# Keys and values of an attention kernel computed with features on partitions, values matmuls unjoined

## The chip, the cores and the metric

The kernel runs on one core of one Trainium2 chip. Its time is the device time of one execution in microseconds (us); the time of a kernel is the median of several executions. Beside it stands one execution recorded by the hardware profiler, whose span is counted from the first to the last instruction.

## The reference

Attention with 16 query heads and one shared head for keys and values, 64 batches of 128 tokens, width 512, head size 64, all in fp32. A null key and a null value stand ahead of each batch's own.

```python
xn = layernorm(x, g_in)
q = (xn @ Wq).reshape(b, n, H, DH).transpose(0, 2, 1, 3) * scale
kv = xn @ Wkv
k, v = (kv[..., :DH], kv[..., DH:])          # one head for all queries
k = jnp.concatenate([nk, k], axis=1)         # null key and null value first
v = jnp.concatenate([nv, v], axis=1)
sim = jnp.einsum('bhid,bjd->bhij', q, k) + bias
# causal mask, then the mask of valid tokens
attn = jax.nn.softmax(sim, axis=-1)
out = jnp.einsum('bhij,bjd->bhid', attn, v)
out = out.transpose(0, 2, 1, 3).reshape(b, n, INNER) @ Wo
return x + layernorm(out, g_out)
```

The kernel subtracts the null key from every key and the null value from every value (so the null score is zero and the null value is added back once at the end). That subtraction is the only arithmetic between the keys' and values' matmuls and their use.

## The kernel before

**Stages.** 64 batches are worked in 16 groups of four and in 32 pairs. A *turn* d handles the pair of batches 2d and 2d+1: `turn(d)` makes their scores on PE (`scores`, L661), adds bias and mask on DVE (`scores_add`), and runs the values matmuls (`values`, L785) of the pair before. Then `body(d)` fills PE with everything else: keys and values for one pair of the next group (`kv_pair`), seven block products that give the next group's queries (`product`, `inner_product`), and seven block products of the output projection for the pair before (`out_product`). Turns 1 to 29 run so; `body_first` is turn 0's, and the last turns have code of their own (`turn_end`, `body_end`, `body_last`). Ahead of turn 0 stands a prologue that computes group 0 (its queries in chunks, `q_half` and `q_batches`), written out step by step at the end of the kernel.

**What sets the order.** The order is written by hand: each engine executes its own instructions in the order in which the program issues them, and the framework adds semaphore waits where two instructions touch the same buffer. Nearly all DMAs are issued on SP's queue, in program order as well. PSUM is handed out by tags with few buffers: `ps_s` "s" (one), `ps_q` "a" and "c", `ps_y` "X" and "Y" (one each) and `ps_w` "w" (two). A product that continues in a room (`start=False`) must wait until the copy of what stands there is done: product 6 on "a" is copied by ACT (`keep`, L551, the tile ku), then product 7 adds into the same "a".

**Keys and values.** For each batch, `kv_mm` (L348) holds the tokens (xT, 128 x 128) as weights and moves the 128 columns of Wkv, four chunks of the contraction. The result has tokens on partitions and 128 features (64 of keys, 64 of values) in the free dimension. `kv_pair` does two batches into two halves of one "s" room; `kv_pair_out` (L395) subtracts the null vectors (broadcast over all partitions, `nkv`) in one DVE operation into `kvt`. In the second pair of each group, that is in odd turns, follow

- `values_to_memory` and `values_spread`: values go to DRAM by three DMAs and come back by four, which put each 32-token block's values on all four quadrants of partitions (`vr`);
- `keys_T`: a DVE transpose of 32 x 32 blocks (L424, `kb`), three DMAs to DRAM and four back into `kT`, with features on partitions, twice (rows 0 to 63 and 64 to 127).

In fp32 each matmul of the program shows as two records in the profile, so a pair's 8 matmuls are 16 records.

**Around the pair in `body`.** On DVE the pair's output comes after the maxima and statistics of other batches and before `pair_nmr` (L943), `norm_stats`, `scores_max`, `inner_out` (L621), and the output of the query products (`q_out`, L560). On ACT, `values_out` (L824) comes before it, then `keep` of product 1 (L551, kp), `pair_norm` (L950, which needs `pair_nmr`'s result), exponentials (L707), `out_keep` (L906), and `keep` of product 6 (L551, ku).

**Values.** `values` works on 32-row quadrants of the array. For each quadrant s there are four positions in `turns`, each with a block of keys j, a target `to` and a count n of blocks. A quadrant named in `wide` joins two matmuls of j = 1 (128 columns each) into one of 256 columns. In turns 2 to 29, quadrant 3 is joined; in turn 1 and in the last turns nothing is.

`PLACE = 0, 1, 3, 2` is the order in which the four 32-token blocks of a batch lie in xT.

Of the kernel before, what the change touches and what calls it, by code (L numbers as in the profile page):

```python
# [8 lines left out]
FP = mybir.dt.float32  # L9
U8 = mybir.dt.uint8  # L10
AF = mybir.ActivationFunctionType
# [6 lines left out]
def kernel(  # L18
# [127 lines left out]
    nkv = const.tile([P, KVN], FP, name="nkv")  # L146
# [115 lines left out]
    xT, qT, kT, vr = {}, {}, {}, {}  # L262
# [85 lines left out]
    def kv_mm(m, pkv=None):  # L348
        g, t = divmod(m, GB)
        if pkv is None:  # L350
            pkv = ps_w.tile([P, KVN], FP, tag="w", name=f"pkv_{m}")
        for kc in range(KC):
            nc.tensor.matmul(  # L353
                pkv,
                xT[g][:, t, kc, :],
                wkv[:, kc, :],
                start=(kc == 0),
                stop=(kc == KC - 1),
            )
        return pkv  # L360

    def kv_pair(m):

        pkv = ps_s.tile([P, 2, DIM], FP, tag="s", name=f"pkv_{m}")
        for i in range(2):
            kv_mm(m + i, pkv[:, i, 0:KVN])
        return pkv

    def to_tokens(out, places):
        for at, to, n in ((0, 0, 2), (2, 3, 1), (3, 2, 1)):  # L370
            nc.sync.dma_start(
                out=out[to * Q : (to + n) * Q], in_=places[at * Q : (at + n) * Q]
            )

    kvts, vds = {}, {}

    def kv_tile(g):
        kvts[g] = hp.tile([P, 2, GB, DH], FP, tag="kv", name=f"kvt_{g}", bufs=1)

    def values_to_memory(g):  # L380
        vds[g] = dp.tile([P, GB * DH], FP, tag="vd", name=f"vd_{g}")
        to_tokens(vds[g], kvts[g][:, 1].rearrange("p t d -> p (t d)"))

    def kv_out(m, pkv):
        g, t = divmod(m, GB)
        if t == 0:
            kv_tile(g)
        nc.vector.tensor_tensor(
            kvts[g][:, :, t, :],
            pkv.rearrange("p (r d) -> p r d", r=2),  # L390
            nkv.rearrange("p (r d) -> p r d", r=2),
            ALU.subtract,
        )

    def kv_pair_out(m, pkv):  # L395
        g, t = divmod(m, GB)
        if t == 0:
            kv_tile(g)
        nc.vector.tensor_tensor(
            kvts[g][:, :, t : t + 2, :],  # L400
            pkv[:, :, 0:KVN].rearrange("p i (r d) -> p r i d", r=2),
            nkv.rearrange("p (r d) -> p r d", r=2)
            .unsqueeze(2)
            .broadcast_to([P, 2, 2, DH]),
            ALU.subtract,
        )
        if t == GB - 2:
            values_to_memory(g)

    def values_spread(g):  # L410

        vd = vds.pop(g)
        vr[g] = hp.tile([P, NQ, GB, DH], FP, tag="vr", name=f"vr_{g}")
        src = vd.rearrange("(j p) e -> p j e", p=Q)
        for s in range(NQ):
            nc.sync.dma_start(
                out=vr[g][s * Q : (s + 1) * Q].rearrange("p j t d -> p j (t d)"),
                in_=src,
            )

    def keys_T(g):

        kb = hp.tile([P, 2, GB, Q], FP, tag="kb", name=f"kb_{g}", bufs=1)
        nc.vector.transpose(  # L424
            kb,
            kvts[g][:, 0].rearrange("p t (c k) -> p c t k", k=Q),
        )
        kd = dp.tile([P, 2, GB * Q], FP, tag="kd", name=f"kd_{g}")
        to_tokens(kd.rearrange("p c e -> p (c e)"), kb.rearrange("p c t q -> p (c t q)"))
        if g == 0:  # L430
            load_mask(0)
        kT[g] = hp.tile([P, NQ, GB, Q], FP, tag="kT", name=f"kT_{g}", bufs=1)
        src = kd.rearrange("(i p) c e -> c p i e", p=Q)
        for s in range(NQ):
            nc.sync.dma_start(
                out=kT[g][s * Q : (s + 1) * Q].rearrange("p i t q -> p i (t q)"),
                in_=src[s % 2],
            )
# [222 lines left out]
    def scores(b, hf, tiles=None):  # L661
# [10 lines left out]
        for f in range(NF):  # L672
            for r in range(2):
                rows = slice(r * DH, (r + 1) * DH)
                for u in range(2):
# [3 lines left out]
                        kT[g][rows, 0 : nk // Q, t, :],  # L679
# [105 lines left out]
    def values(b, wide=()):  # L785
# [8 lines left out]
        for turn in range(len(turns[0])):  # L794
            for s in range(NQ):
# [7 lines left out]
                for r in range(2):  # L803
# [3 lines left out]
                        vr[g][quad, j, t, :],  # L807
# [172 lines left out]
    def turn(d):  # L980
# [16 lines left out]
        values(p, () if d == 1 else (3,))  # L997
        values(p + 1, () if d == 1 else (3,))
# [270 lines left out]
    def body(d):  # L1269
# [258 lines left out]
    q_half(4, 0)  # L1528
# [4 lines left out]
    q_half(5, 0)  # L1533
# [3 lines left out]
    q_half(6, 0)  # L1537
# [3 lines left out]
    q_half(7, 0)  # L1541
# [105 lines left out]
```

## Time and profile before

| | before |
|---|---|
| median of 3 runs | 1028.9 us (1028.81 to 1029.09) |
| profiled execution | 1028.83 us |
| its span | 1027.1 us |
| granted TensorE clock | 1.000 |
| instructions | 31399 |

How to read it. Engines are PE (matmul), PEld (load of weights, which overlaps PE), DVE (VectorE), ACT (ScalarE), POOL (GpSimd) and SP (which issues DMAs; SPq is its queue). L805 is line 805 of the kernel. A row of the timeline has the start, the duration from the first start to the last end of merged instructions, engine, line, operation, tiles written and read, their shapes, the count, and in brackets the idle time of the engine ahead of it and what ended it. Durations of neighbours overlap, since an instruction starts before the one before it has drained; so costs are taken from start to start. A row of groups has count, busy time and mean duration, then idle time and its releaser. A row of one tile has minimum, median and maximum duration. A row of waits has who waited for whom, the total in us, the number of times and the longest. A row of stretches has its length, then PE, PEld, DVE, ACT and POOL busy time with counts, the granted clock, and DMA. A row of DMA issues ends in the median us from issue to landing.

### The profile page before, as it was taken

The numbers are of one execution on the slowest core, as the hardware profiler recorded it, in microseconds if no ns is written. First come the engines' busy times: TensorE is split into PE (matmuls) and PEld (weight loads), VectorE is DVE, ScalarE is ACT, GpSimd is POOL, SyncE is SP. The second block draws the span as 40 slices with busy tenths as digits, with TensorE's granted clock in tenths as the row PEclk, the third lists the DMA queues.
The fourth block names the chain that finished last, engine by engine and source line by source line (L and its number), as shares of the span: only waits on it lengthen the run. The fifth ranks groups of instructions, "written<-read, shape, count | busy, mean of one in ns | idle before, by whom it ended". The sixth has DMA issues, their size and how long they took to land.

```text
span 1027.1 us, 31399 instructions
## 1 busy us (share of the span) xinstructions
PE 1017.6 (99%) x12337; PEld 904.7 (88%) x12337; DVE 787.5 (77%) x1774; ACT 677.5 (66%) x2709; POOL 745.4 (73%) x579
## 2 busy tenths in 40 slices
PE   9999999999999999999999999999999999999997
PEld 8888888888888888898888888888888888888886
DVE  6867777877778877788777778777788777877697
ACT  4756667666677666686656776666776667856582
POOL 4997768686685867758677686766868678586676
PEclk9999999999999999999999999999999999999999
DMA  7514152241613315133151521415223161330211
GB/s 221 167 33 141 63 171 80 71 120 64 181 69 104 97 63 178 63 120 113 40 170 63 160 85 47 150 63 176 75 94 106 58 184 62 109 88 24 94 64 63
DMA packets 69228, 105.14 MB, mean 102 GB/s; under 512 B 9044, under 2 KB 33496, under 8 KB 67288
## 3 DMA queue, kind: packets, MB, share of 16 engines
q1 hardware_dynamic: 68784, 102.73, 31.9%
q8 instruction: 97, 1.59, 0.6%
q14 instruction: 51, 0.42, 0.1%
q10 hardware_dynamic: 296, 0.40, 0.1%
HBM read 67.45 MB, written 35.65 MB: 100 GB/s over the span
## 4 chain that ended last, share of the span: by engine, by line
PE 97%; DVE 1%; POOL 1%; issue 0%; DMA 0%; POOLq 0%; DVEq 0%
PE pa L539 20%; PE pyX L892 20%; PE pyY L892 10%; PE pc L539 10%; PE po L805 7%; PE pkv L353 6%; PE pyw L892 5%; PE pl L605 4%; PE pq L474 3%; PE ps L676 3%; PE sc_X L676 2%; PE sc_Y L676 2%; PE py_s L892 1%; PE sc_a L676 1%; PE sc_w L676 1%
## 5 line engine op out<-in xcount | busy, mean ns | idle before, releaser
L707 ACT ACTIVATE s<-s,nmax 128x65 f32<-128x65 f32 (+1 forms) x1024 | 371.8, 367 | 62.0 <-DVE nmax L698 62.0
L729 POOL TENSOR_TENSOR s<-s,rinv 128x512 f32<-128x512 f32 (+1 forms) x132 | 190.8, 1447 | 156.3 <-DVE rinv L725 156.3
L641 POOL TENSOR_TENSOR s<-biasp,mneg 128x1552 f32<-128x1552 f32 (+1 forms) x65 | 205.8, 3169 | 51.2 <-DVE s L691 38.2
L707 ACT ACTIVATION_READ_ACCUMULATOR s<-s,nmax 128x1 f32 x1024 | 194.2, 190 | 0.0
L557 ACT COPY qT<-pa 128x256 f32<-128x256 f32 x59 | 22.0, 373 | 155.1 <-PE pa L539 155.1
L698 DVE TENSOR_REDUCE nmax<-s 128x8 f32<-128x1032 f32 (+1 forms) x128 | 121.6, 951 | 0.1
L539 PE MATMUL pa<-xS,wq 128*128 128x256 f32 x472 | 121.2, 379 | 0.0
L745 DVE STREAM_TRANSPOSE sb<-s 128x1536 f32<-128x1536 f32 (+1 forms) x68 | 113.6, 1673 | 2.0 <-POOL s L729 2.0
L892 PE MATMUL pyX<-wo,oT 128*128 128x256 f32 x464 | 109.7, 379 | 0.0
L892 PE MATMUL pyX<-wT,oT 128*128 128x256 f32 x464 | 109.7, 379 | 0.0
L539 PEld LDWEIGHTS pa<-xS,wq 128*128 128x128 f32 x472 | 86.4, 190 | 11.9 <-issue 0.2
L892 PEld LDWEIGHTS pyX<-wo,oT 128*128 128x128 f32 x464 | 86.0, 190 | 10.5
L892 PEld LDWEIGHTS pyX<-wT,oT 128*128 128x128 f32 x464 | 85.9, 190 | 10.6
L872 POOL TENSOR_TENSOR oT<-oT 128x512 f32<-128x512 f32 x64 | 80.6, 1279 | 3.9 <-PE pyw L892 1.6
L805 PE MATMUL po<-sb,vr 32*64 32x128 f32 (+1 forms) x3840 | 81.5, 310 | 0.0
L560 DVE TENSOR_TENSOR qT<-pc,ku 128x256 f32<-128x256 f32 x118 | 48.7, 413 | 39.0 <-PE pc L539 22.5
L805 PEld LDWEIGHTS po<-sb,vr 32*64 32x64 f32 x3840 | 71.3, 131 | 8.1 <-issue 5.7
L824 ACT ACTIVATE oT<-po,nv 128x512 f32<-128x512 f32 (+1 forms) x127 | 73.7, 653 | 0.1
L621 DVE TENSOR_TENSOR qT<-pl,kp 128x128 f32<-128x128 f32 x112 | 31.0, 277 | 55.6 <-PE pl L605 53.8
L280 POOL TENSOR_TENSOR rstd<-rstd,nhalf 128x1 f32<-128x1 f32 x64 | 35.4, 560 | 45.9 <-DVE rstd L279 43.7
L353 PE MATMUL pkv<-wkv,xT 128*128 128x128 f32 x512 | 65.2, 281 | 0.0
L551 ACT COPY ku<-pa 128x256 f32<-128x256 f32 x118 | 43.4, 368 | 32.7 <-PE pa L539 24.4
(185 smaller groups left out, 2395.1 us busy)
## 6 DMA issues: line engine op xcount, KB each, us to landing
res<-in_x_dram SPq DMA_DIRECT2D x64, 256.0 KB, 2.9
x<-in_x_dram SPq DMA_DIRECT2D x63, 256.0 KB, 4.5
out_dram<-y SPq DMA_DIRECT2D x63, 256.0 KB, 2.0
xd<-xb SPq DMA_DIRECT2D x14, 1024.0 KB
xT<-xd SPq DMA_DIRECT2D x56, 256.0 KB, 5.9
vr<-vd SPq DMA_DIRECT2D x64, 128.0 KB, 2.7
kT<-kd SPq DMA_DIRECT2D x64, 64.0 KB, 2.2
wo<-in_L_cond_Wo_dram SPq DMA_DIRECT2D x1, 2048.0 KB, 13.5
```

Of the source, the lines that this page charges most:

```text
L353: nc.tensor.matmul(pkv, xT[g][:, t, kc, :], wkv[:, kc, :], start=(kc == 0), stop=(kc == KC - 1),)
L539: nc.tensor.matmul(prod[tag], w[:, kc, f * P : (f + 1) * P], t[:, :, kc, :], start=(start and kc == 0), stop=(kc == HK - 1), skip_group_ch ...
L641: nc.gpsimd.tensor_tensor(S[b][:, :, keys], biasp[:, :, keys], mneg[:, t, keys] .unsqueeze(1) .broadcast_to([P, R8, keys.stop - keys.start ...
L676: nc.tensor.matmul(home[r][u * DH : (u + 1) * DH, f, :], qT[g, f, t // 2][rows, t % 2, hf, u], kT[g][rows, 0 : nk // Q, t, :], start=True, ...
L698: nc.vector.tensor_reduce(nmax[b][:, hf], S[b][:, :, WITH_NULL[hf]], AX.X, ALU.max, negate=True)
L707: nc.scalar.activation(row, row, AF.Exp, bias=nmax[b][:, hf, k : k + 1], accum_out=rsum[b][:, hf, k : k + 1],)
L729: nc.gpsimd.tensor_tensor(sv, sv, rinvs[b, hf][:, lo:hi].unsqueeze(2).broadcast_to([P, hi - lo, sv.shape[2]]), ALU.mult,)
L745: nc.vector.transpose(sbs[b][:, :, lo:hi].rearrange("p j e q -> p e j q"), S[b][:, lo:hi, 1 : ROW - 1].rearrange("p e (j k) -> p e j k", k=Q),
L805: nc.tensor.matmul(po[s][rows, to : to + n], vr[g][quad, j, t, :], sb[quad, slots, r * NF : (r + 1) * NF, :], start=(turn == 0), stop=True ...
L824: nc.scalar.activation(to, src, AF.Identity, bias=nv2)
L872: eng.tensor_tensor(o, a, b, op)
L892: nc.tensor.matmul(prod[key], h[:, c, :], w[:, c, :], start=(start and c == 0), stop=(c == HC - 1), skip_group_check=not start,)
```

## The change

1. **Matmuls of keys and values.** `kv_pair` now holds Wkv's chunk (128 x 128) as weights and moves the tokens of two batches, 256 columns. The result has the 128 features on partitions (keys on rows 0 to 63, values on rows 64 to 127) and the two batches' tokens in the free dimension, in one half of the "s" room. `kv_mm`, `kv_out`, `to_tokens`, `keys_T` and the rest of the old path are gone.
2. **Keys.** They come out as the scores need them. DVE subtracts the null key for token blocks 0 and 1, ACT (two activations with a bias of minus the null key) for blocks 2 and 3, which change places; one DMA copies rows 0 to 63 to rows 64 to 127. `kT` is one tile for all groups.
3. **Values.** DVE subtracts the null value on rows 64 to 127 into `vTs`; once a group DVE transposes 32 x 32 blocks of these 64 rows x 512 columns (`values_T`), two DMAs write them to DRAM in pieces of 32 features, four bring them back into `vr`.
4. The null vectors are loaded as one value per partition instead of a broadcast row, and `null_negative` computes the negative once.
5. **Values matmuls**: quadrant 3 is no longer joined.
6. **Prologue**: the second pair of group 0 is done as a pair, in a `ps_w` room; query chunks 3 to 7 of the first half use `q_batches` (per batch, 128 columns) instead of `q_half` (256 columns); `load_mask(0)` is issued ahead of `values_T(0)`.

```diff
-    nkv = const.tile([P, KVN], FP, name="nkv")
+    nkv = const.tile([P, 1], FP, name="nkv")
+    nkv_neg = const.tile([P, 1], FP, name="nkv_neg")
...
-            out=nkv, in_=cond[0:2].rearrange("r d -> (r d)").partition_broadcast(P)
+            out=nkv, in_=cond[0:2].rearrange("r d -> (r d)").unsqueeze(1)
...
+    K_ROWS, V_ROWS = slice(0, DH), slice(DH, P)
+    kT = hp.tile([P, NQ, GB, Q], FP, tag="kT", name="kT", bufs=1)
+    vTs = {}
+
+    def kv_pair(m, room=None):
...
+        if room is None:
+            two = ps_s.tile([P, 2, DIM], FP, tag="s", name=f"pkv_{m}")
+            pkv = two[:, 0, 0 : 2 * N]
+        else:
+            pool, tag = room
+            pkv = pool.tile([P, 2 * N], FP, tag=tag, name=f"pkv_{m}")
         for kc in range(KC):
             nc.tensor.matmul(
                 pkv,
-                xT[g][:, t, kc, :],
                 wkv[:, kc, :],
+                xT[g][:, t : t + 2, kc, :],
...
     def kv_pair_out(m, pkv):
         g, t = divmod(m, GB)
         if t == 0:
-            kv_tile(g)
-        nc.vector.tensor_tensor(
-            kvts[g][:, :, t : t + 2, :],
...
+            vTs[g] = hp.tile([P, GB, N], FP, tag="kv", name=f"vT_{g}", bufs=1)
+        two = slice(t, t + 2)
+        nc.vector.tensor_scalar(
+            vTs[g][V_ROWS, two],
+            pkv[V_ROWS].rearrange("p (t n) -> p t n", t=2),
+            nkv[V_ROWS],
+            None,
             ALU.subtract,
         )
...
+        src = pkv[K_ROWS].rearrange("p (t i q) -> p t i q", t=2, i=NQ)
+        out = kT[K_ROWS, :, two].rearrange("p i t q -> p t i q")
+        nc.vector.tensor_scalar(
+            out[:, :, 0:2], src[:, :, 0:2], nkv[K_ROWS], None, ALU.subtract
+        )
+        for i in (2, 3):
+            nc.scalar.activation(
+                out[:, :, i], src[:, :, PLACE[i]], AF.Identity, bias=nkv_neg[K_ROWS]
+            )
+        nc.sync.dma_start(out=kT[V_ROWS, :, two], in_=kT[K_ROWS, :, two])
+
+    def values_T(g):
+
+        vb = hp.tile([P, GB * NQ, Q], FP, tag="vb", name=f"vb_{g}", bufs=1)
+        nc.vector.transpose(
+            vb[V_ROWS], vTs[g][V_ROWS].rearrange("p t (j q) -> p (t j) q", q=Q)
+        )
+        vd = dp.tile([Q, GB * NQ, DH], FP, tag="vd", name=f"vd_{g}")
+        for at in range(0, DH, Q):
+            nc.sync.dma_start(
+                out=vd[:, :, at : at + Q], in_=vb[DH + at : DH + at + Q]
+            )
+        vr[g] = hp.tile([P, GB, NQ, DH], FP, tag="vr", name=f"vr_{g}")
         for s in range(NQ):
             nc.sync.dma_start(
...
+                out=vr[g][s * Q : (s + 1) * Q].rearrange("p t j d -> p (t j) d"),
+                in_=vd,
             )
...
-        values(p, () if d == 1 else (3,))
-        values(p + 1, () if d == 1 else (3,))
+        values(p)
+        values(p + 1)
...
             if h == 1:
-                keys_T(g)
-                values_spread(g)
+                values_T(g)
...
-    pkvs = [kv_mm(m) for m in (2, 3)]
+    pkv2 = kv_pair(2, (ps_w, "w"))
     norm_stats(5)
     norm_stats(6)
+    null_negative()
     kv_pair_out(0, pkv)
     norm_stats(7)
     causal(1)
-    q_half(3, 0)
-    for m in (2, 3):
-        kv_out(m, pkvs[m - 2])
-    keys_T(0)
-    values_to_memory(0)
-    values_spread(0)
+    q_batches((3,))
+    kv_pair_out(2, pkv2)
+    load_mask(0)
+    values_T(0)
...
-    q_half(4, 0)
+    q_batches((4,))
...
-    q_half(5, 0)
+    q_batches((5,))
...
-    q_half(6, 0)
+    q_batches((6,))
...
-    q_half(7, 0)
+    q_batches((7,))
```

The scores read `kT` without the group's index, and `values` reads `vr[g][quad, t, PLACE[j], :]` instead of `vr[g][quad, j, t, :]`.

More of the change, by code (lines that the diff above doesn't have):

```diff
@@ L260 @@
     dp = ctx.enter_context(tc.tile_pool(name="dp", bufs=2, space=bass.MemoryType.DRAM))
-    xT, qT, kT, vr = {}, {}, {}, {}
+    xT, qT, vr = {}, {}, {}
     stats = {}
@@ L360, in kv_mm, with null_negative @@
         return pkv
[L362 to L386, printed above, removed]
-            kv_tile(g)
[L388 to L393, printed above, removed]
+    def null_negative():
+        nc.vector.tensor_scalar(nkv_neg, nkv, -1.0, None, ALU.mult)
     def kv_pair_out(m, pkv):
@@ L397, in kv_pair_out @@
         if t == 0:
-            kv_tile(g)
-        nc.vector.tensor_tensor(
-            kvts[g][:, :, t : t + 2, :],
[L401 to L404, printed above, removed]
+            vTs[g] = hp.tile([P, GB, N], FP, tag="kv", name=f"vT_{g}", bufs=1)
[5 more added lines that the diff above has]
+            None,
@@ L415, in values_spread @@
         for s in range(NQ):
             nc.sync.dma_start(
[L417 to L437, printed above, removed]
+                out=vr[g][s * Q : (s + 1) * Q].rearrange("p t j d -> p (t j) d"),
@@ L678, in scores @@
                         qT[g, f, t // 2][rows, t % 2, hf, u],
-                        kT[g][rows, 0 : nk // Q, t, :],
+                        kT[rows, 0 : nk // Q, t, :],
                         start=True,
```

11 lines of the change are left out of this document (1 added, 10 removed).

## The prediction

> **What bounds the kernel now.** I read the page first, its busy shares and its chain of work, then the waits of PE, then two stretches of one turn's length.
>
> ```profile
> PE 1017.6 (99%) x12337; PEld 904.7 (88%) x12337; DVE 787.5 (77%) x1774; ACT 677.5 (66%) x2709; POOL 745.4 (73%) x579
> PE 97%; DVE 1%; POOL 1%; issue 0%; DMA 0%; POOLq 0%; DVEq 0%
> ```
>
> ```profile
> PE py_s L892 <- DVE oT L822: 1.4, 2, 0.8
> PE busy L1478 <- POOL neg L244: 1.4, 1, 1.4
> ```
>
> ```profile
> 91.46:122.76 31.30, 31.30 (x384) 27.85 (x382) 24.05 (x55) 20.63 (x83) 25.92 (x22) 1.00 0.19 68
> 500.00:531.30 31.30, 31.30 (x394) 27.91 (x386) 24.45 (x57) 20.78 (x84) 21.05 (x15) 1.00 0.50 145
> ```
>
> PE is busy for 99% of the span and is 97% of the chain. Its longest waits are 1.4 us each, at the start and in the last turns. In the middle a turn of two batches takes 31.30 us, and PE is busy in all of it (the second number), at clock 1.00; DVE has about 24 and ACT about 21. So a saved PE nanosecond is a saved nanosecond, and work on DVE, ACT, POOL or a queue costs nothing until it holds back a matmul. Two questions follow: what the change does to PE's own time, and which hand-over between engines has less slack than the change eats.
>
> **PE's own time.** Starts of consecutive groups give true costs, since the durations overlap.
>
> ```profile
> 8.75 5.52 PE L474 MATMUL pq<-xT,wq 128*128 128x128 f32 x48
> 14.11 1.04 PE L312 MATMUL pxT<-ident,x 128*128 128x128 f32 x8
> 14.98 3.74 PE L353 MATMUL pkv<-wkv,xT 128*128 128x128 f32 x32
> 18.55 3.62 PE L474 MATMUL pq<-xT,wq 128*128 128x256 f32 x16
> 22.01 0.60 PE L312 MATMUL pxT<-ident,x 128*128 128x128 f32 x4
> 22.45 1.89 PE L474 MATMUL pq<-xT,wq 128*128 128x256 f32 x8
> ```
>
> ```profile
> 63.12 2.52 PE L805 MATMUL po<-sb,vr 32*64 32x256 f32 x128
> 65.57 1.16 PE L353 MATMUL pkv<-wkv,xT 128*128 128x128 f32 x8
> ...
> 188.47 2.54 PE L805 MATMUL po<-sb,vr 32*64 32x256 f32 x120
> 190.94 2.05 PE L353 MATMUL pkv<-wkv,xT 128*128 128x128 f32 x16
> 192.83 1.03 PE L539 MATMUL pa<-xT,wq 128*128 128x256 f32 x4
> ```
>
> - Keys and values. A pair of batches now takes 16 matmul records 128 wide, afterwards 8 records 256 wide. Narrow: 32 from 14.98 to 18.55 is 3.57 us, 0.1117 each, 1.787 for 16 (pq gives the same: 5.36/48). Wide: 16 from 18.55 to 22.01 is 3.46, 0.216 each, 1.73 for 8. Saved: 0.057 per pair. In a turn the block takes 1.89 and not 1.79, because the first load of weights behind the values matmuls is exposed (0.10); it stays exposed, so the saving is the same. 32 pairs: 32 x 0.057 = **-1.82 us**.
> - Values unjoined. Turn 1 already runs unjoined: 128 records, 63.12 to 65.57, 2.45 us. Turn 5 is joined: 120 records, 188.47 to 190.94, 2.47. Eight more matmuls make the block shorter, as far as rows of hundredths can say by 0.01 to 0.02. I take 0.015, for the 28 turns that are joined now (2 to 29): **-0.42 us**.
> - Queries of the prologue. Five chunks (3 to 7) go from 8 records 256 wide to 16 that are 128 wide: 5 x 0.057 = **+0.29 us**.
>
> Sum on PE alone: -1.95 us.
>
> [...]
>
> **What DVE does more.** Today a pair is one subtraction on DVE, and each second turn (the odd ones) adds the transpose of keys. Afterwards it is two tensor_scalars and, in odd turns, a transpose of twice the width.
>
> ```profile
> 193.03 0.43 DVE L399 TENSOR_TENSOR kvt<-pkv,nkv 128x256 f32<-128x256 f32 x1 [0.61 <-PE pkv L353]
> 193.49 0.45 DVE L424 STREAM_TRANSPOSE kb<-kvt 128x256 f32<-128x256 f32 x1
> 193.86 0.29 DVE L943 TENSOR_SCALAR nmro<-mvo,rstdo 128x1 f32<-128x1 f32 x2
> ...
> 201.84 0.68 DVE L956 TENSOR_TENSOR y<-yn,res 128x512 f32<-128x512 f32 x1
> 202.56 0.42 DVE L560 TENSOR_TENSOR qT<-pc,ku 128x256 f32<-128x256 f32 x1
> 202.90 1.29 DVE L325 STREAM_TRANSPOSE xb<-x 128x512 f32<-128x512 f32 x2
> ```
>
> ```profile
> L399 DVE TENSOR_TENSOR kvt<-pkv,nkv x31: 411/425/426, 18.2 to 944.2; 128x256 f32<-128x256 f32 x31
> L388 DVE TENSOR_TENSOR kvt<-pkv,nkv x2: 281/281/281, 19.5 to 19.7; 128x128 f32<-128x128 f32 x2
> ```
>
> ```profile
> 973.50 1.66 DVE L822 TENSOR_SCALAR oT<-po,nv 128x256 f32<-128x256 f32 x4 [0.83 <-PE po L805]
> ```
>
> The nearest row to the new tensor_scalars is L822: PSUM to SBUF with a per-partition scalar, four 256-wide in 1.66, so 0.39 from start to start (the last ends 0.47 after its start). For 128 wide I take 0.25, which is 0.39 less the 0.14 between the medians of the 256-wide and the 128-wide subtraction (425 and 281 ns). Two of L325, 512 wide, take 1.29, the second 0.68: 0.61 from start to start. DVE starts at 192.96 instead of 193.03, as PE is 0.07 earlier (0.057 and 0.015). It reaches L943 at 192.96 + 0.39 + 0.25 + 0.61 = 194.21 instead of 193.86: **0.35 late in odd turns**. That 64 partitions in place of 128 change nothing is my choice; the bounds are no lateness at all (they cost half: 193.59) and 0.6 (each of the three by its whole duration, 0.47 + 0.33 + 0.68 from 192.96, is 194.44, and 0.02 more).
>
> ```profile
> 224.33 0.42 DVE L399 TENSOR_TENSOR kvt<-pkv,nkv 128x256 f32<-128x256 f32 x1 [0.60 <-PE pkv L353]
> 224.67 0.33 DVE L943 TENSOR_SCALAR nmro<-mvo,rstdo 128x1 f32<-128x1 f32 x2
> ```
>
> In even turns, without a transpose, L943 follows 0.34 behind the pair's start; with 0.39 + 0.25 from a start 0.07 earlier it comes 0.23 late.
>
> **Who notices.** Two hand-overs lie close behind.
>
> ```profile
> 191.13 2.39 ACT L824 ACTIVATE oT<-po,nv 128x512 f32<-128x512 f32 x4
> 193.95 0.37 ACT L551 COPY kp<-pa 128x256 f32<-128x256 f32 x1 [0.43 <-PE pa L539]
> 194.22 0.79 ACT L950 ACTIVATE yn<-y,nmro,rstdo 128x512 f32<-128x512 f32 x1
> ...
> 196.27 0.35 ACT L906 COPY kyp<-pyX 128x256 f32<-128x256 f32 x1
> 196.76 0.37 ACT L551 COPY ku<-pa 128x256 f32<-128x256 f32 x1
> ```
>
> ```profile
> 197.37 1.03 PE L539 MATMUL pa<-xS,wq 128*128 128x256 f32 x4
> ...
> 203.44 1.03 PE L539 MATMUL pc<-xS,wS 128*128 128x256 f32 x4
> ```
>
> First, ACT's pair_norm (L950) needs the first result of L943. It comes at 194.21 + 0.20 + 0.03 = 194.44, so pair_norm starts 0.22 late, and all behind it on ACT. ACT had slack: it was free for the ku copy at 196.54 (0.27 after 196.27) and began at 196.76, waiting for PE. Now it begins at 196.76 and ends at 197.13. PE's product 7 writes over what this copy reads; its first matmul would start at 197.37 - 0.07 = 197.30 and needs the copy done 0.16 before, at 197.14 (0.05 for the semaphore, and 0.11 for a load of weights, the spacing of narrow matmuls). 197.13 just makes it. Second, q_out (L560): DVE was free for it at 201.84 + 0.61 = 202.45, now 202.80; it ends at 203.22. Product 5 of the next chunk wants it 0.16 before 203.37, that is at 203.21. **A stall of about 0.02 us in 14 odd turns (3 to 29): +0.3 us**, between none and 0.26 a turn (3.6 us) by the bounds. In even turns there is room: the 0.23 is less than the 0.49 us of idle time ahead of the same q_out.
>
> ```profile
> 233.86 0.42 DVE L560 TENSOR_TENSOR qT<-pc,ku 128x256 f32<-128x256 f32 x1 [0.49 <-PE pc L539]
> ```
>
> ACT's two new activations (Identity with a bias, 64 elements per partition from PSUM) fall into the 0.43 us in which ACT waits for PE before 193.95.
>
> ```profile
> L707 ACT ACTIVATE s<-s,nmax 128x65 f32<-128x65 f32 x512 | 171.8, 339 | 62.0 <-DVE nmax L698 62.0
> ```
>
> Their price lies between 0.07 (64 of the 512 that each L824 does in 0.57, the same operation) and 0.34 (the whole duration of an activation 65 wide). I take 0.12, near the first. ACT is free at 191.13 + 4 x 0.57 = 193.41 and again at 193.65; kp can start at 193.88. Hidden, with 0.23 to spare; with that cover gone see the last rival.
>
> At nothing I also put:
> - the DMAs: a group goes from 14 to 8; keys get their second half by one copy inside SBUF, values still go through DRAM, now in 128-byte pieces. On SP's queue the key copy waits for DVE and ACT, and the mask load and the stores wait behind it. Keys are next read a turn later, values two turns later.
>
> ```profile
> vr<-vd SPq DMA_DIRECT2D x64, 128.0 KB, 2.7
> kT<-kd SPq DMA_DIRECT2D x64, 64.0 KB, 2.2
> ```
>
> Both are medians from issue to landing. Against 20 us or more (a turn of 31.30 less its first third) they could grow fivefold unnoticed; past that, PE would wait for the rest at the next scores.
>
> The one kT for all groups is free as well: a turn's scores have read the batches that the pair then overwrites, and PE runs scores before the pair. In the prologue DVE gets about 0.4 us later by the same prices; PE has query chunks to run there (22.45 and on), and without them it would cost those 0.4 us once.
>
> **Sum.** -1.82 - 0.42 + 0.29 + 0.3 = -1.65 us. The profiled execution took 1028.83 (span 1027.1 and 1.7 around it), 0.07 under the median of 1028.9. Forecast 1028.83 - 1.65 = **1027.2 us**, own range 1026.8 to 1028.0. Differences under 0.2% (2.06 us) count as no change, about what a measurement of this kernel can tell.
>
> **Rivals.**
> - No stall, or a larger gain: -1.95 and up to 0.2 more if the values save 0.02. 1026.7. For it: both margins come out within 0.03. Against: nothing in the rows saves more.
> - The narrow step is smaller than the kv rows say: four pxT, also 128 wide, take 0.44 (22.01 to 22.45), 0.110 each; then a pair saves 0.03. -0.96 - 0.42 + 0.15 = -1.2: 1027.6. [...] Against: the kv rows themselves are measured.
> - Odd turns stall for 0.1 to 0.26, as DVE's new work is dearer: 14 times, +1.4 to +3.6 on -1.95: 1028.3 to 1030.5.
> - **Slower**: ACT's activations land on the path in every turn. They write the same kT as DVE's second tensor_scalar; if they have to wait for it (it ends at about 193.7) and cost the 0.34 of L707 each, ACT is free at 194.43, kp is 0.48 later than 193.95, and ku is free at 197.02 and done at 197.39: 0.25 after 197.14, in 28 turns, +7.0 us. 1033.9. The point from which PE stalls at all is an end after 194.18; from 194.25 on (0.07 x 28 = 1.95) nothing is left of the gain. For it: ACT runs in order, and pair_norm, the exps and ku stand behind. Against: DVE and ACT write different parts of kT, and L824 is the nearer row.
>
> **Chances.** Forecast 0.48, of which 0.05 falls under 1026.84; larger gain 0.17 (0.16 of it under that line); narrow step, by row or rule, 0.05; odd stalls 0.10; slower 0.20. Faster by over 0.2%: 0.05 + 0.16 = 0.21; within 0.2%: 0.43 + 0.01 + 0.05 + 0.10 = 0.59; slower: 0.20. The range for 8 in 10 goes from 1026.5 to 1032.0, which takes in the bounds of the odd turns and the near side of the slower rival.
>
> **What would show it.** pkv: 256 records, 8 in 1.83 us behind the values; po to pkv 2.45 in each turn; even turns 31.23 us long (31.30 less 0.07). In odd turns the load for product 7 and that for product 5 of the second chunk show their delay. Wrong would be: an even turn longer than 31.30, a wait of PE on ACT or DVE in the list of waits that was not there, or kv activations that end more than 3.2 us after the pkv group starts (194.18 on this scale).

## The result, and the profile after

The changed kernel takes **1035.31 us** (median of 6 runs, 1035.17 to 1035.54) where the kernel before takes 1028.95 beside it (6 runs): 6.4 us more, a ratio of 1.0062 with a 95% interval of 1.0049 to 1.0075. The forecast was 1027.2, its range 1026.5 to 1032.0. The profiled execution took 1035.41, with a span of 1033.6 at clock 1.00.

The page of the kernel after, engines and chain:

```profile
PE 1021.9 (99%) x12345; PEld 895.9 (87%) x12345; DVE 805.6 (78%) x1806; ACT 689.1 (67%) x2773; POOL 744.8 (72%) x579
...
PE 90%; ACT 4%; DVE 3%; issue 1%; POOL 1%; DMA 0%; POOLq 0%; DVEq 0%; ACTq 0%
```

PE still looks 99% busy, since the records of matmuls overlap (four take 1.03 us where the next four start 0.86 later) and so cover a part of each wait. The chain is the better witness: PE had 97% of it, now 90%, and ACT has come in with 4%, DVE with 3 (1 before). The list of waits names the place; first PE's, then those of its loads of weights (what waits, for what, us in total, times, longest):

```profile
PE pa L515 <- ACT ku L527: 2.3, 14, 0.2
```

```profile
PEld pa L515 <- ACT ku L527: 7.9, 14, 0.6
...
PEld pa L515 <- POOL rstd L281: 3.9, 13, 0.3
```

PE's wait was not there before. L515 is the matmul of `product` and L527 the copy in `keep` (the old L539 and L551): product 7 waits for ACT's copy ku in 14 turns. The 13 waits put down to POOL are the same load in the even turns: it waits for ACT and for POOL, and POOL's result had been there 0.14 us before ACT's (turn 6: 229.82 and 229.96).

By windows from one pkv group to the next, the odd turn 5 and the even turn 6 of the kernel after (after the window: its length, PE's busy time, the other engines'):

```profile
191.98:223.64 31.66, 31.50 (x387) 27.55 (x383) 25.17 (x58) 21.03 (x86) 21.68 (x16) 1.00 0.48 141
223.64:255.03 31.39, 31.39 (x387) 27.55 (x383) 24.45 (x57) 21.95 (x88) 23.59 (x20) 1.00 0.17 57
```

Before, both took 31.30. Odd turns lose 0.36 us, even ones 0.09; 14 of each are 6.3 us. Turn 1 is 0.08 shorter, and the prologue 0.6 longer by the start of turn 1. Measured from the pkv group of turn 5, PE is 0.06 ahead of the old kernel until product 7, 0.27 behind when product 7 starts and 0.37 behind when it is done; from there on the distance stays, to 0.02. In turn 6 it is 0.06 ahead, then 0.03 and 0.10 behind. So the whole loss of a turn arises at one hand-over.

The timeline of turn 5 after, ACT (start, duration, instruction, and in brackets the idle time before it and what ended it):

```profile
192.19 2.39 ACT L800 ACTIVATE oT<-po,nv 128x512 f32<-128x512 f32 x4
194.98 0.51 ACT L393 ACTIVATE kT<-pkv,nkv_neg 64x64 f32<-64x64 f32 x2 [0.40 <-DVE kT L389]
195.38 0.35 ACT L527 COPY kp<-pa 128x256 f32<-128x256 f32 x1
195.96 0.78 ACT L926 ACTIVATE yn<-y,nmro,rstdo 128x512 f32<-128x512 f32 x1 [0.22 <-DVE nmro L919]
...
198.26 0.36 ACT L527 COPY ku<-pa 128x256 f32<-128x256 f32 x1
```

DVE in the same stretch:

```profile
194.02 0.49 DVE L380 TENSOR_SCALAR vT<-pkv,nkv 64x256 f32<-64x256 f32 x1 [0.53 <-PE pkv L363]
194.54 0.34 DVE L389 TENSOR_SCALAR kT<-pkv,nkv 64x128 f32<-64x128 f32 x1
194.91 0.71 DVE L401 STREAM_TRANSPOSE vb<-vT 64x512 f32<-64x512 f32 x1
195.65 0.33 DVE L919 TENSOR_SCALAR nmro<-mvo,rstdo 128x1 f32<-128x1 f32 x2
```

And PE:

```profile
191.98 1.99 PE L363 MATMUL pkv<-xT,wkv 128*128 128x256 f32 x8
193.81 1.03 PE L515 MATMUL pa<-xT,wq 128*128 128x256 f32 x4
...
197.49 1.03 PE L515 MATMUL pc<-xS,wS 128*128 128x256 f32 x4
198.68 1.13 PE L515 MATMUL pa<-xS,wq 128*128 128x256 f32 x4 [0.16 <-ACT ku L527]
199.65 1.89 PE L868 MATMUL pyw<-wo,oT 128*128 128x256 f32 x8
```

Two things are to be seen. ACT sits idle for 0.40 us and starts its activations only when DVE's keys operation (L389) is done. And each of DVE's operations starts when the one before it has ended, and not ahead of that end: 194.02 + 0.49 = 194.51, and L389 starts at 194.54; 194.54 + 0.34 = 194.88, and the transpose starts at 194.91; 194.91 + 0.71 = 195.62, and L919 starts at 195.65. Start to start that is 0.52, 0.37 and 0.74 us. The prediction had priced 0.39, 0.25 and 0.61.

In the even turn 6, which has no transpose, the keys operation waits in the same way (225.67 + 0.49 = 226.16, and it starts at 226.19), but L919 does not: like the keys operation ahead of it, it begins at partition 0, and it starts 0.07 before that one has ended.

```profile
225.67 0.49 DVE L380 TENSOR_SCALAR vT<-pkv,nkv 64x256 f32<-64x256 f32 x1 [0.53 <-PE pkv L363]
226.19 0.34 DVE L389 TENSOR_SCALAR kT<-pkv,nkv 64x128 f32<-64x128 f32 x1
226.46 0.32 DVE L919 TENSOR_SCALAR nmro<-mvo,rstdo 128x1 f32<-128x1 f32 x2
```

**Theory.** DVE operations that begin at another partition (64 of 128) than their neighbours do not overlap, 0.13 us each (0.52, 0.37 and 0.74 here, 0.39, 0.25 and 0.61 priced); and ACT's activations wait until DVE has read the PSUM room pkv, and so come late too. Both delay pair_norm (L926), and with it ku, which had no slack. **Rivals**: half-height operations are slower by themselves; ACT's work alone does it; the wait has to do with kT, which both engines write.

In what follows a turn's length is the median over the trace's even or odd turns from the second on, from pkv group to pkv group. The kernel before, on the same chip as each set of runs, took 1029.05 to 1029.20 us (medians).

### The profile page after: what moved, and what is told of

It is laid out like the page before. It is cut to its first block, busy times and chain, and to the rows that moved or that the text cites. A ratio compares the mean times of both kernels' runs of the same rounds, so it can differ in the third digit from the quotient of the medians.

```text
span 1033.6 us, 31331 instructions
## 1 busy us (share of the span) xinstructions
PE 1021.9 (99%) x12345; PEld 895.9 (87%) x12345; DVE 805.6 (78%) x1806; ACT 689.1 (67%) x2773; POOL 744.8 (72%) x579
## 3 DMA queue, kind: packets, MB, share of 16 engines
q8 instruction: 96, 1.57, 0.7%
## 4 chain that ended last, share of the span: by engine, by line
PE 90%; ACT 4%; DVE 3%; issue 1%; POOL 1%; DMA 0%; POOLq 0%; DVEq 0%; ACTq 0%
PE pa L515 18%; PE pyX L868 17%; PE pyY L868 10%; PE pc L515 9%; PE po L781 7%; PE pkv L363 6%; PE pyw L868 5%; PE pl L581 4%; PE pq L450 3%; PE ps L652 3%; PE sc_X L652 2%; ACT s L683 2%; PE sc_Y L652 2%; PE py_s L868 1%; PE sc_a L652 1%
## 5 line engine op out<-in xcount | busy, mean ns | idle before, releaser
L515 PE MATMUL pa<-xS,wq 128*128 128x256 f32 x472 | 123.8, 385 | 2.3 <-ACT ku L527 2.3
L515 PEld LDWEIGHTS pa<-xS,wq 128*128 128x128 f32 x472 | 85.1, 190 | 21.6 <-ACT ku L527 7.9
L781 PE MATMUL po<-sb,vr 32*64 32x256 f32 (+1 forms) x4064 | 81.0, 300 | 0.0
L781 PEld LDWEIGHTS po<-sb,vr 32*64 32x64 f32 x4064 | 70.9, 130 | 8.1 <-issue 5.7
L597 DVE TENSOR_TENSOR qT<-pl,kp 128x128 f32<-128x128 f32 x112 | 31.1, 277 | 55.5 <-PE pl L581 53.8
L363 PE MATMUL pkv<-xT,wkv 128*128 128x256 f32 x256 | 63.3, 391 | 0.0
L515 PE MATMUL pc<-xS,wS 128*128 128x256 f32 x236 | 60.6, 379 | 0.0
```

Of the source, the lines that this page charges most:

```text
L363: nc.tensor.matmul(pkv, wkv[:, kc, :], xT[g][:, t : t + 2, kc, :], start=(kc == 0), stop=(kc == KC - 1),)
L515: nc.tensor.matmul(prod[tag], w[:, kc, f * P : (f + 1) * P], t[:, :, kc, :], start=(start and kc == 0), stop=(kc == HK - 1), skip_group_ch ...
L781: nc.tensor.matmul(po[s][rows, to : to + n], vr[g][quad, t, PLACE[j], :], sb[quad, slots, r * NF : (r + 1) * NF, :], start=(turn == 0), st ...
```

## Experiments

### e1_full_rows: all 128 partitions for the values

```
-            vTs[g][V_ROWS, two],
-            pkv[V_ROWS].rearrange("p (t n) -> p t n", t=2),
-            nkv[V_ROWS],
+            vTs[g][:, two],
+            pkv.rearrange("p (t n) -> p t n", t=2),
+            nkv,
...
-            vb[V_ROWS], vTs[g][V_ROWS].rearrange(...)
+            vb, vTs[g].rearrange(...)
```

> Values' subtraction and transpose work on all 128 partitions (rows 0 to 63, which nothing reads, take along the keys). Same free sizes. Theory (DVE operations that begin on another partition than the one before wait until that one has finished, so the pair costs 0.52 + 0.37 + 0.74 us instead of 0.39 + 0.26 + 0.61): the three come back to about 0.39, 0.26 and 0.61 from start to start, L919 begins 0.38 us earlier in odd turns, ACT's activations 0.13 earlier; even turns 31.26, odd turns about 31.28, total near 1028.2. Rival (operations with a scalar operand on 64 rows are slow in themselves, or the ku hand-over is not behind it): spacing as in the changed kernel, 1035.3.

Measured: **1027.69 us** (1027.51 to 1028.39), ratio to before 0.9986 (0.9977 to 0.9996). Even turns 31.26, odd turns 31.26. DVE works on twice as many rows, and the whole loss is gone. Its DVE rows in turn 5:

```profile
193.79 0.48 DVE L380 TENSOR_SCALAR vT<-pkv,nkv 128x256 f32<-128x256 f32 x1 [0.53 <-PE pkv L363]
194.19 0.33 DVE L389 TENSOR_SCALAR kT<-pkv,nkv 64x128 f32<-64x128 f32 x1
194.45 0.69 DVE L401 STREAM_TRANSPOSE vb<-vT 128x512 f32<-128x512 f32 x1
195.07 0.29 DVE L919 TENSOR_SCALAR nmro<-mvo,rstdo 128x1 f32<-128x1 f32 x2
```

Start to start 0.40, 0.26, 0.62: the prediction's prices to 0.01. The keys operation is the same 64 rows in both kernels; only its neighbours have changed, and with them its step, from 0.37 to 0.26. So what counts here is not the height but that all now begin at partition 0.

### e2_late_transpose: the transpose of the values later

```
-            if h == 1:
-                values_T(g)
...
+        if q and h == 1:
+            values_T(g)
         if soft:
```

The second place is just ahead of the exponentials that follow in `body`.

> values_T moved in the same body from behind the pair to just ahead of exps(a, 1, 4), where DVE idles. Theory (odd turns are longer than even ones because the transpose keeps DVE from L919, which pair_norm on ACT needs, which keeps ku from PE): odd turns 31.32, about as even ones (31.39), total near 1030.6. Rival (the DMAs of the values or the stall at the second hand-over, q_out to product 5, make the odd turns): odd turns stay at 31.5 or more, total over 1033.

Measured: **1031.04** (1030.94 to 1031.23). Odd turns 31.32 as the theory has it, even ones 31.39, unchanged since they have no transpose. Turn 1 took 32.10, 0.71 more than in the changed kernel, once (0.4 of it is a wait of PE on DVE's qT), and the prologue was 0.23 shorter (turn 1 starts at 65.93, not 66.16); together these are the 0.4 that the total lies above the expected 1030.6. The odd turns' extra is the transpose and what it holds.

### e3_keys_on_act and e4_keys_on_dve: who makes the keys

```
e3:
-        nc.vector.tensor_scalar(
-            out[:, :, 0:2], src[:, :, 0:2], nkv[K_ROWS], None, ALU.subtract
+        nc.scalar.activation(
+            out[:, :, 0:2], src[:, :, 0:2], AF.Identity, bias=nkv_neg[K_ROWS]
e4:
-            nc.scalar.activation(
-                out[:, :, i], src[:, :, PLACE[i]], AF.Identity, bias=nkv_neg[K_ROWS]
+            nc.vector.tensor_scalar(
+                out[:, :, i], src[:, :, PLACE[i]], nkv[K_ROWS], None, ALU.subtract
```

> ACT does the keys' blocks 0 and 1 too, in a third activation; DVE's keys operation is gone. Theory (not ACT's own 0.4 us, but its start behind DVE's last read of the same PSUM room delays it): ACT can start when DVE's one values operation is done, 0.37 earlier; kp 0.1 earlier although ACT does more; even turns about 31.30, odd turns 31.28, total near 1028.7. Rival (ACT's own work is the price): about 0.28 us more work, even turns 31.6 or more, total about 1039.

> DVE does all of the keys (blocks 2 and 3 in two more operations of 64 columns), ACT nothing of the pair. Theory (even turns are ACT's, odd turns DVE's): even turns 31.26, odd turns longer, about 31.95, since the transpose comes 0.3 later still; total near 1037.5. Rival (the activations on ACT make both kinds of turn long): both at 31.23, total near 1027.

Measured: e3 **1030.03** (1029.72 to 1030.15), even turns 31.23, odd 31.41. e4 **1039.66** (1039.05 to 1040.39), even 31.23, odd 32.04. That more work on ACT helps (e3) refutes the rival that ACT's own work is the load. In e4 the even turns gain too, as ACT waits for nothing of the pair, and the odd ones lose, as the transpose and L919 come later still on DVE; its total lies 2.2 above the expected, 1.3 of it by odd turns 0.09 longer than expected and 1.1 behind the last of these turns. In e3, where DVE writes nothing of kT, the first activation still starts when DVE's reading of pkv for the values has ended, ACT and then DVE:

```profile
193.94 0.36 ACT L389 ACTIVATE kT<-pkv,nkv_neg 64x128 f32<-64x128 f32 x1
```

```profile
193.41 0.49 DVE L380 TENSOR_SCALAR vT<-pkv,nkv 64x256 f32<-64x256 f32 x1 [0.54 <-PE pkv L363]
```

193.41 + 0.49 = 193.90, and ACT starts 0.04 later. ACT's own values_out would have let it start at about 193.89 here, so turn 5 alone does not settle it. The prologue of e3 does: there ACT has been idle for 0.81 us, its bias nkv_neg is written by 17.86, and it starts 0.04 after DVE's reading of pkv has ended (17.89 + 0.49 = 18.38).

```profile
18.42 0.36 ACT L389 ACTIVATE kT<-pkv,nkv_neg 64x128 f32<-64x128 f32 x1 [0.81 <-DVE vT L380]
```

```profile
17.72 0.14 DVE L373 TENSOR_SCALAR nkv_neg<-nkv 128x1 f32<-128x1 f32 x1
17.89 0.49 DVE L380 TENSOR_SCALAR vT<-pkv,nkv 64x256 f32<-64x256 f32 x1
```

So the room that both read is enough for the wait; that both write kT is not needed for it.

e3's odd turns were 0.13 longer than expected, and pair_norm, at 3.61 us after pkv, does not explain that. Block by block against e1, PE loses 0.03 at product 7 and 0.12 at a later product into the room pc, whose reader, a DVE operation, comes 0.15 late. DVE loses those 0.12 in one step, from one row to the next (e3, turn 5):

```profile
196.94 1.22 DVE L674 TENSOR_REDUCE nmax<-s 128x8 f32<-128x1032 f32 x1
198.19 0.29 DVE L597 TENSOR_TENSOR qT<-pl,kp 128x128 f32<-128x128 f32 x1
```

That is 1.25 us, the whole duration of the maximum and 0.03; the same two operations stand 1.13 apart in e1 and in the kernel after. What differs on DVE is which operation last read PSUM before L597: in e3 the values subtraction at partition 64, in e1 and in the kernel after the keys operation at partition 0. In odd turns ten operations lie between (the transpose, L919's two, statistics and a maximum, none of which reads PSUM). That the last read of PSUM makes these 0.12 us is the author's reading; no run tries it alone.

### e5_full_keys_on_act: e1 and e3 together

> The values op and the transpose on all 128 partitions, and all keys by ScalarE, none by VectorE. Theory (what is left in the full-rows run is the two activations' wait for VectorE's keys op, worth 0.03 us a turn at product 7): pair_norm starts about 3.5 us after pkv, no stall in either kind of turn, both 31.23, 1026.9 us. Nothing is held at L597 now, because the last PSUM read of VectorE before it begins at partition 0 again, so the 0.115 us of the odd turns of the keys-on-ScalarE run must be gone as well. Rival (the three activations delay ScalarE by themselves, as in that run's odd turns): odd turns 31.40, 1029.4 us.

Measured: **1027.60** (1027.45 to 1028.27), ratio 0.9988 (0.9979 to 0.9997). All turns from the second on take 31.23, even and odd: the kernel's own PE time with no stall at all, 0.07 under the old 31.30. The 0.13 us of e3's odd turns (31.41, of which 31.28 were expected) is gone too, as expected with values operations that begin at partition 0. The total is 0.7 above the 1026.9 expected; turn 1 takes 31.59 (0.2 of it), and the rest lies outside the turns.

### e7_transpose_64 and e8_values_64: one of the two on full rows

e7 is e1 with the transpose back on the upper 64 rows; e8 has the transpose on 128 rows, whose lower half is zeros written once, and the values operation on 64.

> The values op on all 128 partitions, the transpose still on the upper 64 only. Theory (a VectorE operation that begins at another partition than the one before starts only when that one has finished, and so does the next): the transpose starts 2.81 and the nmro op 3.55 us after pkv in the odd turns, pair_norm 3.81; odd turns 31.50, even ones 31.26 as with both on full rows, 1031.0 us. Rival (only the number of partitions counts, or only the values op was at fault): odd turns 31.26, 1027.7 us.

> The values op still on the upper 64 partitions, the transpose on all 128 (the lower rows of its input are zeros written once). Theory: keys op held to 2.54 us after pkv, transposes then at 2.80 and nmro at 3.42 in the odd turns; the activations 2.96, so pair_norm 3.64 to 3.70: even turns 31.39, odd turns 31.33 to 31.38, 1030.5 us. Rival (the transpose alone was at fault): even 31.26, odd 31.26, 1027.7 us.

Measured: e7 **1031.51** (1031.36 to 1032.58), odd turns 31.53, even 31.26. e8 **1031.09** (1030.96 to 1031.65), odd 31.39, even 31.39. Both are as the theory has them, and neither operation alone is at fault. e7's DVE rows show who is held, the operation that begins elsewhere and the next one:

```profile
193.88 0.33 DVE L389 TENSOR_SCALAR kT<-pkv,nkv 64x128 f32<-64x128 f32 x1
194.24 0.71 DVE L401 STREAM_TRANSPOSE vb<-vT 64x512 f32<-64x512 f32 x1
194.98 0.33 DVE L919 TENSOR_SCALAR nmro<-mvo,rstdo 128x1 f32<-128x1 f32 x2
```

0.36 and 0.74 from start to start, against 0.26 and 0.62 in e1.

### e6_full_act_qhalf: the third term undone, and a surprise

e5 with `q_half(c, 0)` in place of `q_batches((c,))` for the five chunks 3 to 7.

> The run before with the five chunks of queries of the prologue as q_half, as they were before the change. Theory (the prediction's third term, 5 x 0.057): 0.29 less than the run before it, 1026.6 us, turns unchanged. Rival (the prologue waits for something else, a load or the norms): no difference, 1026.9 us.

Measured: **1036.76** (1035.35 to 1037.63), 9 us *more* than e5, where theory and rival had 0.3 less or nothing. In the prologue the term is there: from the first query chunk to the first one behind turn 0's scores the trace is 0.289 us shorter than e5's, 5 x 0.058. But from then on the values block (L781), which nothing in the edit touches, takes 2.6 to 3.0 us in each turn and not 2.45. The loads of weights of the values block ahead of turn 6's pkv group, e5 and then e6:

```profile
219.88 2.28 PEld L781 LDWEIGHTS po<-sb,vr 32*64 32x64 f32 x128 [0.17 <-issue]
```

```profile
221.67 1.09 PEld L781 LDWEIGHTS po<-sb,vr 32*64 32x64 f32 x54 [0.17 <-issue]
223.00 1.35 PEld L781 LDWEIGHTS po<-sb,vr 32*64 32x64 f32 x74 [0.24 <-issue]
```

In e5 one run of 128, in e6 a hole of 0.24 us after 54 of them, "issue": the engine waited for nothing that the profile shows. By the list of waits of e6 there are 10.9 us of it in 50 places (the kernel after has 5.7 and e5 5.5, in 32 places: the 0.17 ahead of each block):

```profile
PEld po L781 <- issue: 10.9, 50, 0.5
```

What can 20 products fewer at the start (4 in each of the five chunks) do to turn 28? They move the block's place in TensorE's program. The page of e6 has a queue of instructions:

```profile
q8 instruction: 96, 1.57, 0.7%
```

96 loads of 16 KB each (1.57 MB / 96). That they bring TensorE's program is inferred: in the trace of the kernel after, 255 matmul and weight-load records of PE begin on average from one load to the next. At 64 bytes an instruction (an estimate: 1.57 MB over the 24,610 matmul and weight-load records of PE is 64) one load holds 256 instructions, and the values block (128 matmuls, 128 weight loads) uses up as many in 2.45 us, where an average load lasts about 11 (1035.5 / 96). A turn has 764 such instructions (382 matmuls and as many loads of weights), and the trace of e5 has 5 semaphore instructions beside them in even turns and 3 in odd ones: 768 on average, by the same estimate three loads exactly, so a load falls at about the same place in every turn. In the kernel after one begins 3.1 to 3.9 us ahead of the values block and the next 0.5 to 1.2 us into it (turns 1 to 29). In turn 6 of e5 one begins 0.6 us into the block and none in the 1.3 us ahead of it; in turn 6 of e6 one begins 1.4 us ahead and the next 2.4 us into it. **New theory:** the block's place in these loads makes the hole, and the kernels before (a load 2.0 to 3.9 us ahead of the block, which takes 2.45 to 2.47) and after (2.45) both stand at a place without one.

### e9 to e12: is it the place?

The narrow products of these runs are 32x32 by 4 columns into the room of the warming products, `keep_busy(4, narrow=20)` and so on; nobody reads them.

```
+        for _ in range(narrow):
+            nc.tensor.matmul(
+                pb[0:Q, 0:4], ident[0:Q, 0:Q], ident[0:Q, 0:4], start=True, stop=True
+            )
```

e12 is e5 with the values joined as before:

```
-        values(p)
-        values(p + 1)
+        values(p, () if d == 1 else (3,))
+        values(p + 1, () if d == 1 else (3,))
```

> The q_half run (full rows, keys on ScalarE, five q_half; its values block has a hole of about 0.3 us at its 52nd record in most turns) with 20 narrow products (32x32 by 4 columns, into the room that the warming products write, read by nobody) put into the prologue's third warming group, so that TensorE's program has as many products ahead of the turns as with q_batches. Theory (the place of the values block in TensorE's instruction loads of 16 KB decides, and the 20 products fewer had moved it): the hole is gone, the block takes 2.45 again, turns 31.23, 1026.6 plus up to 0.8 for the 20 products. Rival (q_half itself, its order or its rooms, makes the hole): turns 31.65, 1036.8 or more.

> The run with full rows and keys on ScalarE (q_batches, no hole) with 44 such narrow products. 44 products of 4 instructions are 176, which is 80 short of one load of 256 instructions, the same place as 20 products fewer. Theory (place): holes as in the q_half run, turns 31.6, 1036 to 1038. Rival (not the place): turns 31.23, 1027.6 plus up to 1.8.

> The kernel before, otherwise untouched, with 48 such narrow products, which put its values block at the place of the q_half run's. Theory (place): the kernel before gets the hole too, turns 31.6 to 31.75, 1036 to 1041. Rival (the hole needs something of the change): turns 31.30, 1029 plus up to 1.9.

> The run with full rows and keys on ScalarE, with the values products joined again from the second turn on, as before the change: 4 products fewer in a turn, so 16 instructions, and the block moves by 16 of 256 from turn to turn. Theory (place): the turns are no longer alike, a hole of 0.1 to 0.5 us in perhaps a third of them and none in the others, 1029 to 1032. Rival (the prediction's second term read the other way, 0.015 a turn): turns 31.24, all alike, 1028.0.

| run | edit | us | turns (even, odd) | values block |
|---|---|---|---|---|
| e9 | e6 + 20 products | 1028.92 (1028.55 to 1029.19) | 31.23, 31.23 | 2.45 in all turns |
| e10 | e5 + 44 products | 1040.96 (1039.03 to 1042.17) | 31.66, 31.41 | 2.45 to 3.23 |
| e11 | before + 48 products | 1038.20 (1035.39 to 1039.18) | 31.49, 31.39 | 2.47 to 3.12 |
| e12 | e5, values joined | 1031.61 (1030.78 to 1034.08) | 31.36, 31.24, up to 31.77 | 2.47 to 2.99 |

Twenty products that compute nothing make the kernel 8 us faster (e9 against e6), and 48 make the old one 9 us slower. Not all of the 9 is the hole: turn 1 starts 3.6 later (69.16, before 65.57), and turns 2 to 28 together are 5.0 longer (850.1, before 845.1). In e10 the prologue is 3.6 longer as well (turn 1 starts at 69.48, in e5 at 65.83), which is why its total lies 3 above the expected 1036 to 1038; its turns 2 to 28 are 9.2 longer. e10 is the sharpest of the four: by loads of 256 instructions (the estimate above), 44 products more are the same place as 20 fewer, and the hole came. e9's block is the same in every turn again. It does not reach the 1026.6 plus 0.8: the prologue with the narrow products is 1.2 us longer than e5's (start of turn 1 at 67.04 and 65.83). e12 moves the block by 16 instructions a turn and so tries the places one after another: in the seven turns in which a load begins 3.7 to 2.7 us ahead of the block it takes 2.45 to 2.47; of the 22 in which one begins 1.8 to 0.3 us ahead, 13 are longer by 0.14 to 0.53. With no hole e12's turns take 31.24, 0.015 more than e5's: the prediction's second term.

That the place in the program makes the hole is shown (8 us between e6 and e9); that it counts by loads of 256 instructions, an estimate, rests on e10 and on the order of e12's turns. Why a hole arises there is not: in e10, e11 and e12 some turns at such a place have none, so something else, perhaps how long a load took (not measured), must come in.

## Why the prediction was wrong, by its steps

- **PE's own time: right.** The pkv group takes 1.83 (before 1.89), 223.64 to 225.47 in turn 6; the values block 2.45 in every turn (turn 5's was 2.47 before); a turn without a stall 31.23. Five chunks of queries cost 0.29. The rival by the narrow pxT step is out: a pair saves 0.057. For the "rule" that the chances name beside that row no run shows anything; what the runs showed in its place is the pkv group 0.06 shorter.
- **The hand-over: right place.** "ku copy, then product 7" is where all of the stall arises. The limit that the slower rival named, activations that end later than 3.24 us after the start of pkv, was right too: kp follows them at 3.40 (195.38 - 191.98), and in even turns, where pair_norm waits for kp and not for L919, the stall is the difference, 0.16 (31.39 against 31.23).
- **The step that failed first: "that 64 partitions in place of 128 change nothing is my choice".** DVE's three operations cost 1.63 and not 1.25 in odd turns, as each begins at a partition where the one before did not. That made L919 0.4 later than the forecast's already late one, and pair_norm with it: it starts 3.98 after pkv, predicted 3.51. The stall predicted for odd turns was 0.02; 0.43 was measured. The upper bound, each operation by its whole duration, had this mechanism but not its size: it puts L919 0.6 late, and from the start of pkv it came 0.75 late (3.67, before 2.92), as each operation took 0.01 to 0.03 more and 0.03 lies between two. Its price of 0.26 a turn is that of q_out, which stalled in no turn of the kernel after; by the same rows the ku copy would have cost about 0.24 (an estimate: pair_norm 0.47 late, ku done at 197.38 and wanted at 197.14). In the DVE rows of the changed kernel, e1, e3, e4, e7 and e8 each of these operations that begins at another partition than the one before it starts 0.01 to 0.04 us after that one's end, and each other one 0.06 to 0.09 ahead of it, unless it uses the result of the one before (e3's transpose, 0.04 after); e3's 0.12 us at L597 stands apart from them, and its cause is not shown. With 0.03 from each end to the next start the prediction's rows would have given 0.50, 0.36 and 0.71 (an estimate: their whole durations and 0.03 each); 0.52, 0.37 and 0.74 were measured.
- **The second step that failed: "Hidden, with 0.23 to spare".** ACT was free for its activations 2.49 us after pkv (192.19 + 4 x 0.57 - 191.98) and started them at 3.00, waiting for DVE. They cost 0.40 for the two and not 0.24, which alone would still have been hidden (2.49 + 0.40 is 2.89, and kp started at 3.01 before). The kernel reads one PSUM room from two engines, and the second reader waits for the first: ACT starts 0.10 after DVE's keys operation has ended (194.98 and 194.88). With the wait, kp starts 3.40 after pkv. The two steps work together: with no operation held the wait costs 0.03 a turn (e1, 31.26 against 31.23), and where ACT does not wait for the keys operation the even turns lose nothing (e3 and e4, 31.23). So of the stalls of 0.43 and 0.16, all but 0.03 need the held operations, which makes the first step the main one.
- **The slower rival** (chance 0.20) was this mechanism, for the wrong reason: a wait for "the same kT". The room explains e3, where DVE writes nothing of kT; whether the shared kT would make ACT wait by itself no run shows. Its price of 0.25 in 28 turns was 0.16 in even turns and, with DVE's part on top, 0.43 in odd ones: 14 x 0.16 + 14 x 0.43 = 8.3, less PE's own gain, against 7.0.
- **The prologue: partly wrong.** "PE has query chunks to run there" did not hold to the end: PE stalls once for 0.2 us at the scores ahead of turn 0's query chunk, in the changed kernel and in e7, not in e1 to e6 and e8. It waits for DVE's reading of the room ps (L669, 33.93 + 1.23 = 35.16; PE goes on at 35.21). That the held operations make DVE late there is not shown: e2 has the very same prologue and no stall, and its L669 starts at 33.40, 0.53 earlier. Another 0.16 is a later start of PE's work on queries and keys, and this too is not the change: among e1 to e8 and e12, whose work on PE up to there is the same, it lies between 0.11 earlier and 0.55 later than before.
- **The DMAs at nothing: right.** No wait on vr or kT appears in PE's list, though packets under 512 bytes go from 9044 to 32212.
- **Not seen at all**: that two parts of the change, the unjoined values (16 instructions more in a turn, as many as the new keys and values save) and the prologue's q_batches, keep the values block at its place in the instruction loads (one begins 3.1 to 3.9 us ahead of it in the kernel after, 2.0 to 3.9 before). Taken alone either costs 4 to 9 us to undo (e12, e6); the prediction priced them at -0.42 and +0.29.

## What to carry to other kernels

Let neighbouring VectorE operations begin at the same partition, even if half of the rows are computed for nothing: on a path with no slack 0.11 to 0.12 us each (0.52, 0.37 and 0.74 from start to start, in e1 0.40, 0.26 and 0.62) was worth 7.6 us here (1035.31 against e1's 1027.69). Count one PSUM room read by two engines as a chain, not as parallel work: ACT sat idle for 0.40 us here until DVE had read it. And before judging an edit that changes the number of matmuls, look whether a dense block elsewhere has kept its length: its place in the instruction loads moved the time by 8 us here (e6 and e9, which differ by 20 products that nobody reads).

## What the runs showed of the hardware that was not expected

- Of the VectorE operations behind pkv, one that begins at another partition than the one before started 0.01 to 0.04 us after that one's end (kernel after: L389 at 194.54, 0.03 after 194.02 + 0.49); without that, and with nothing to wait for, it started 0.06 to 0.09 before that end (e1: L389 at 194.19, 0.08 before 193.79 + 0.48). In e3 L597, behind a maximum of 1.22 us, came 0.12 later (1.25 against 1.13). The late start alone is no proof of it: an operation that uses the result of the one before also starts 0.03 after that one's end (kernel before, turn 5: 193.03 + 0.43 = 193.46, L424 at 193.49).
- Instructions came in loads of 16 KB (96 in e6), with a median of 1.1 us each in the trace of the kernel after; the values block, 256 instructions in 2.45 us (by the estimate of 64 bytes each, one load), had a hole at some places in them (e6, e10, e11, e12) and not at others (e5, e9), and the hole, 0.1 to 0.5 us, came and went with 20 products of the prologue (e6, e9).
- All 128 partitions cost VectorE no more than 64 here (e1 and the kernel after): 0.48 and 0.49 us for the 256-wide subtraction, 0.69 and 0.71 for the transpose.
